# Exponentials added by fours in every attention block

## The chip, the cores and the metric

The kernel runs on one core of one Trainium2 chip. The metric is the device time of one execution in microseconds (us); the time of a kernel is the median of its runs. The engines are TensorE (PE, with its weight loads as PEld), VectorE (DVE), ScalarE (ACT), GpSimd (POOL) and SyncE (SP), which issues DMAs.

## The reference

One pre-layernorm transformer layer in float32, on x of 2 x 1024 x 1024 (2 sequences of 1024 tokens, width 1024), with 32 heads of width 32 and a gated FFN of width 2752:

```python
x = x + attention(layernorm(x))        # softmax(q k^T / sqrt(32)) v per head, then ctx @ ow + ob
h = layernorm(x)
x = x + (silu(h @ W_gate.T) * (h @ W_up.T)) @ W_down.T
```

## The kernel before

**Blocks and units.** Queries are worked on in four blocks of 512: two sequences, two halves each. A *unit* is two heads of one block; a block has 16 units, and `phase` is the number of the block (0 to 3). The keys of a sequence are eight tiles of 128, `kt` = 0 to 7. For each key tile a unit has one buffer `p[kt]` of 128 keys x 1024 (two heads x 512 queries).

**The steps of a unit.** `scores(i)` (L510) makes the scores of two key tiles in psum. DVE keeps a running maximum of them (`largest`, L526), and ACT copies them to `p[kt]` (`keep`, L529). `maximum` turns the maxima into one number per query (L549, L550, a transpose on TensorE at L564, the negated maximum at L565), which goes through DRAM into the tile `m`. Then, tile by tile, `less_maximum` adds `m` to `p[kt]` (L580; on POOL but for some tiles of block 0), `exponential` takes the exponential in place on ACT (L589), and `add` adds an earlier tile's exponentials (L603).

**The additions.** Instead of a sum p0 v0 + p1 v1 the kernel makes p0 (v0 - v1) + (p0 + p1) v1. `differences` replaces v0 by v0 - v1 on POOL (L594), and `add` replaces p1 by p0 + p1. The softmax's denominators are then sums of every second `p`, and half of the matmuls on a column of ones fall away. In block 0 this is done a second time: p3 becomes the sum of four tiles, v1 becomes v1 - v3 (L597), and only tiles 3 and 7 are multiplied by ones. In blocks 1 to 3 tiles 1, 3, 5 and 7 are (`summed`). In those blocks the additions of tiles 1 and 5 are on POOL and those of 3 and 7 on DVE; in block 0 all are on DVE.

**The values.** `values(kt)` (L618) multiplies `p[kt]` by `v`, and for summed tiles by ones, into the psum tile `acc`. A set is four matmuls of 32 output partitions and 256 columns, each of them two instructions on the chip. Values are issued in runs of four tiles (`RUN`), when the last addition of the run has been issued.

**What runs beside attention.** In block 0 it is the projections of q, k and v (L370, L432). Beside block n the output projection (L780) and the FFN of block n - 1 are worked on: gate and up products in groups of four matmuls of 256 columns (L922), down projections in groups of two of 512 columns (L1071), both in a Strassen-like form of seven products. Each group fills one psum tile from a ring of three (`lin`), and DVE or ACT adds it to its place (L936 to L949, L1084, L1086).

**Order.** All instructions are emitted by the program itself. `Emitter` keeps a planned clock: each matmul step adds its planned cost (`MM4` = 855 ns for 512 columns), and the steps of attention are spread evenly over the steps beside them, 128 *beats* to a block. `em.later(d, f)` emits f once the planned clock is d ns on. After `less_maximum(kt)` the exponential comes 3500 ns later and the addition 8100 ns later; in block 0 the second addition comes at 9900 ns. Values follow the run's last `less_maximum` by three beats. The engines take their instructions in the emitted order.

## Time and profile before

| | us |
|---|---|
| median of 3 runs (lowest to highest) | 3282.67 (3280.46 to 3286.37) |
| the profiled execution, and its span | 3281.96, 3280.2 |
| busy: PE, DVE, POOL, ACT | 3217.5, 1920.4, 1758.6, 1431.2 |
| score maxima on DVE, L526 (384 + 64 instructions) | 468.1 + 77.3 |
| values on TensorE, L618, tiles `vals` and `ones` | 266.0, 137.7 |

Busy time is the union of an engine's instructions; the ends of matmuls are modelled and neighbours overlap, so for TensorE the distance from one start to the next tells more than a duration. An arrow in a row (`<-DVE top L526`) names what ended the idle time ahead of those instructions.

### The profile page before, as it was taken

To read this page: it belongs to the slowest core of one execution; us is meant where nothing else is said; L and a number is where in the kernel's file an instruction comes from. 1 tells how busy PE (TensorE), PEld (TensorE's weight loads), DVE (VectorE), ACT (ScalarE), POOL (GpSimd) and SP (SyncE) were. 2 spreads that over 40 slices of the span, in tenths; PEclk is the share of its full clock that TensorE was granted. 3 is DMA by queue.
4 is the path that set the end of the run, shared out by engine and by line. 5 is a ranking of instruction groups with operands and counts; after the bars stand their busy time and mean duration, and the time that the engine had idled before them with its cause. 6 is when DMAs were issued, how large, how long until landed. Compare 5 with 4: busy or idle time off the path is not lost. (4 is left out here: it accounts for less than half of the span.)

```text
span 3280.2 us, 43732 instructions
## 1 busy us (share of the span) xinstructions
PE 3217.5 (98%) x16320; PEld 1801.1 (55%) x16320; DVE 1920.4 (59%) x2478; ACT 1431.2 (44%) x1570; POOL 1758.6 (54%) x871
## 2 busy tenths in 40 slices
PE   8999999999999999999999999989999999999999
PEld 4444444444347655663466556634655566477775
DVE  2265676666356766666666666676666664344334
ACT  2244554444455545563655455545555554010000
POOL 0267776876676655568665555667765665200000
PEclk9999999999999999999999999999999999999999
DMA  4556766655534445446344444463444444544442
GB/s 155 171 184 193 226 192 203 200 180 161 158 99 135 142 151 146 146 146 200 107 142 145 139 141 137 145 192 110 137 145 146 146 138 140 184 151 153 153 152 97
DMA packets 337826, 507.29 MB, mean 155 GB/s; under 512 B 105424, under 2 KB 122064, under 8 KB 337616
## 3 DMA queue, kind: packets, MB, share of 16 engines
q1 hardware_dynamic: 281424, 405.91, 40.3%
q10 hardware_dynamic: 56192, 98.60, 9.8%
q8 instruction: 130, 2.13, 0.3%
q14 instruction: 80, 0.66, 0.1%
HBM read 429.14 MB, written 75.24 MB: 154 GB/s over the span
## 5 line engine op out<-in xcount | busy, mean ns | idle before, releaser
L580 POOL TENSOR_TENSOR p<-p,m 128x1024 f32<-128x1024 f32 x480 | 1180.8, 2483 | 13.6 <-DMA m<-d 13.4
L529 ACT COPY p<-s 128x1024 f32<-128x1024 f32 x512 | 516.7, 1011 | 872.1 <-DVE top L526 664.5
L526 DVE TENSOR_TENSOR top<-s,top 128x1024 f32<-128x1024 f32 x384 | 468.1, 1219 | 289.0 <-PE s L510 280.0
L589 ACT ACTIVATE p<-p 128x1024 f32<-128x1024 f32 x512 | 532.2, 1057 | 234.7 <-POOL p L580 206.8
L922 PE MATMUL p<-sum,m 128*128 128x256 f32 x2688 | 617.8, 383 | 4.9 <-DVE sum L904 3.3
L603 POOL TENSOR_TENSOR p<-p,p 128x1024 f32<-128x1024 f32 x96 | 227.2, 2367 | 658.9 <-ACT p L589 598.3
L922 PEld LDWEIGHTS p<-sum,m 128*128 128x128 f32 x2688 | 503.2, 190 | 124.7 <-issue 43.0
L922 PE MATMUL p<-xn2T,m 128*128 128x256 f32 x2016 | 473.5, 384 | 1.9 <-ACT gate L934 1.3
L370 PE MATMUL pq<-xnT,wqk 128*128 128x512 f32 x1024 | 463.7, 601 | 0.0
L1071 PE MATMUL pd<-wp,h 128*128 128x512 f32 x960 | 442.3, 607 | 8.3 <-DVE x L1084 6.4
L922 PEld LDWEIGHTS p<-xn2T,m 128*128 128x128 f32 x2016 | 378.2, 191 | 98.5 <-issue 45.4
L603 DVE TENSOR_TENSOR p<-p,p 128x1024 f32<-128x1024 f32 x192 | 306.2, 1595 | 134.1 <-ACT p L589 134.0
L370 PEld LDWEIGHTS pq<-xnT,wqk 128*128 128x128 f32 x1024 | 187.2, 190 | 252.8 <-issue 249.0
L1071 PEld LDWEIGHTS pd<-wp,h 128*128 128x128 f32 x960 | 179.3, 193 | 242.5 <-issue 203.4
L510 PE MATMUL s<-q,k 32*128 32x512 f32 x2048 | 300.8, 645 | 7.1 <-ACT p L529 7.0
L1084 DVE TENSOR_TENSOR x<-pd,x 128x512 f32<-128x512 f32 x360 | 236.9, 681 | 86.8 <-PE pd L1071 86.7
L618 PE MATMUL acc<-p,vals 128*32 128x256 f32 x4096 | 266.0, 383 | 1.8 <-DVE p L603 1.8
L1184 POOL TENSOR_TENSOR ws<-raw 128x512 f32<-128x512 f32 x62 | 93.7, 1512 | 299.9 <-DMA raw<-in_w_gu 170.5
L432 PE MATMUL pvv<-wv,xnT 128*128 128x512 f32 x512 | 233.3, 600 | 1.5 <-ACT xnT L266 1.5
L780 PE MATMUL po<-wo,ctx 128*128 128x512 f32 x512 | 234.6, 607 | 0.0
L618 PEld LDWEIGHTS acc<-p,vals 128*32 128x32 f32 x4096 | 120.1, 110 | 143.6 <-issue 70.2
L950 ACT ACTIVATE gate<-gate 128x512 f32<-128x512 f32 x84 | 52.9, 630 | 278.4 <-DVE gate L949 278.0
(96 smaller groups left out, 2451.3 us busy)
## 6 DMA issues: line engine op xcount, KB each, us to landing
m<-dws SPq DMA_DIRECT2D x336, 256.0 KB
m<-in_w_gu SPq DMA_DIRECT2D x252, 256.0 KB
wp<-ddn SPq DMA_DIRECT2D x160, 256.0 KB
m<-d SPq DMA_DIRECT2D x64, 512.0 KB
wp<-in_w_dn SPq DMA_DIRECT2D x120, 256.0 KB
raw<-in_w_gu ACTq DMA_DIRECT2D x84, 256.0 KB
dws<-ws ACTq DMA_DIRECT2D x84, 256.0 KB
x<-in_x SPq DMA_DIRECT2D x32, 512.0 KB
```

The costliest lines, as they stand in the source:

```text
L370: nc.tensor.matmul(ps, wqk[b, g, w, hk][:, k, :], xnT[b, s][:, kc, :], start=(kc == 0), stop=(kc == KC - 1),)
L510: nc.tensor.matmul(ps[a][:, h * NH : (h + 1) * NH], self.k[rows, i * P : (i + 1) * P], self.q[rows, :], start=True, stop=True,)
L526: nc.vector.tensor_tensor(self.top, s, self.p[0] if kt == 1 else self.top, ALU.max)
L529: nc.scalar.copy(self.p[kt], s)
L580: eng.tensor_tensor(p, p, self.m, ALU.add)
L589: nc.scalar.activation(self.p[kt], self.p[kt], AF.Exp, scale=SCALE)
L603: eng.tensor_tensor(self.p[kt], self.p[kt], self.p[kt - back], ALU.add)
L618: nc.tensor.matmul(self.acc[j * HD : (j + 1) * HD, c : c + NQ], w(h), self.p[kt][:, q0 : q0 + NQ], start=start, stop=stop, skip_group_chec ...
L780: nc.tensor.matmul(st["ps"], ctxT[b, blk][:, g, t * P : (t + 1) * P], st["w"][hf, g], start=(g == 0), stop=(g == G - 1),)
L922: nc.tensor.matmul(ps, mats[c, n][:, kc, :], rhs, start=(kc == 0), stop=(kc == hk - 1),)
L1071: nc.tensor.matmul(st["pd"], lefts[n](pi)[:, j, t * P : (t + 1) * P], st["wp", pi, n, j], start=(j == 0), stop=(j == PART // 2 - 1),)
L1084: nc.vector.tensor_tensor(xs, st["pd"], xs, op)
```

## The change

Tiles are added by fours in all four blocks: the second addition, the second difference of `v` and the fewer ones matmuls no longer depend on the phase. The second addition, `add(kt, 2)` for tiles 3 and 7, stands on DVE, since `add` puts tiles 3 and 7 there in every block. The line numbers after `add` move up by four.

```diff
             if kt % 2 == 1:
-                twice = self.phase == 0 and kt % 4 == 3
+                twice = kt % 4 == 3
                 em.later(8100.0, lambda: self.add(kt, 1), None if twice else ("added", self.n, kt))
                 if twice:
                     em.later(9900.0, lambda: self.add(kt, 2), ("added", self.n, kt))
...
             nc.gpsimd.tensor_tensor(v[:, :, 0, :], v[:, :, 0, :], v[:, :, 1, :], ALU.subtract)
-            if self.phase == 0:
-                v = self.v.rearrange("p (i a) n -> p i a n", a=4)
-                nc.gpsimd.tensor_tensor(v[:, :, 1, :], v[:, :, 1, :], v[:, :, 3, :], ALU.subtract)
+            v = self.v.rearrange("p (i a) n -> p i a n", a=4)
+            nc.gpsimd.tensor_tensor(v[:, :, 1, :], v[:, :, 1, :], v[:, :, 3, :], ALU.subtract)
...
-        def summed(self, kt):
-            return kt % (4 if self.phase == 0 else 2) == (3 if self.phase == 0 else 1)
...
-            if self.summed(kt):
+            if kt % 4 == 3:
                 columns(lambda h: ones, NQ, False, kt == NT - 1)
...
-                    cost = MM4 / 2 * (1 + units[k].summed(v))
+                    cost = MM4 / 2 * (1 + (v % 4 == 3))
                     q.add(lambda k=k, v=v: units[k].values(v), cost)
```

## The prediction

> **What bounds the kernel now.** I read the page's first part for shares, then busy time by stage (the windows view), then the timeline of TensorE around one attention step, then the groups by shape, then the runs of down-projection matmuls, where VectorE is fullest.

> ```profile
> PE 3217.5 (98%) x16320; PEld 1801.1 (55%) x16320; DVE 1920.4 (59%) x2478; ACT 1431.2 (44%) x1570; POOL 1758.6 (54%) x871
> ...
> 130.00:900.00 770.00, 763.48 (x3472) 316.32 (x3471) 458.98 (x425) 364.14 (x400) 540.30 (x286) 1.00 0.61 190
> 900.00:1530.00 630.00, 621.23 (x3582) 370.25 (x3581) 409.43 (x544) 334.29 (x357) 390.28 (x185) 0.99 0.48 143
> 1530.00:2180.00 650.00, 627.61 (x3650) 370.05 (x3649) 431.14 (x555) 345.19 (x369) 405.33 (x190) 0.99 0.47 142
> 2180.00:2822.00 642.00, 631.00 (x3614) 374.57 (x3614) 400.62 (x545) 328.34 (x351) 398.98 (x187) 0.99 0.48 145
> 2822.00:3280.00 458.00, 454.35 (x1667) 313.88 (x1665) 182.61 (x340) 27.40 (x54) 17.97 (x15) 1.00 0.45 145
> ```

> The window columns are length, then busy time and instructions of PE, PEld, DVE, ACT, POOL, then granted clock, DMA share, GB/s. The first window shown is the attention of the first block, which runs beside the projections; the next three are the attention of the other three blocks, each beside the output projection and FFN of the block before; the last has no attention. The edit touches the three middle windows alone, 1922 us. There TensorE is busy 621, 628 and 631 us, at a clock of 0.99, and is without work for 9, 22 and 11 us. DVE is busy 65%, 66% and 62%, POOL 62%. So TensorE's own work sets the length, with VectorE the next.

> ```profile
> 1719.20 1.07 PE L618 MATMUL acc<-p,vals 128*32 128x256 f32 x16
> 1720.09 0.61 PE L618 MATMUL acc<-p,ones 128*32 128x256 f32 x8
> 1720.52 1.05 PE L618 MATMUL acc<-p,vals 128*32 128x256 f32 x16
> 1721.39 0.61 PE L618 MATMUL acc<-p,ones 128*32 128x256 f32 x8
> 1721.93 1.98 PE L1071 MATMUL pd<-wp,h 128*128 128x512 f32 x4
> ```

> This is one run of four key tiles. The durations overlap, so cost is read from start to start: a set of 8 instructions on ones takes 1720.52 - 1720.09 = 0.43 us (0.431 by the records in ns), the 16 on values 0.89.

> **The part removed.** A unit is two heads of one block and has two such runs; three blocks of 16 units have 96 runs. Each run loses its first ones set: 96 x 0.431 = 41.4 us of TensorE. The built order agrees: ones matmuls fall from 896 to 512 in the program, 1792 to 1024 on the chip, where each is two instructions. They stand in TensorE's queue between value matmuls and nothing runs under them, so all of it lies on the path. The planner subtracts the same work (half of MM4 per set), so the 128 beats of a block come 13.8 / 128 = 0.11 us closer.

> **The part added.** 96 additions of 128x1024 on DVE, `add(kt, 2)`, and 48 subtractions of 128x128 on POOL.

> ```profile
> L580 POOL TENSOR_TENSOR p<-p,m 128x1024 f32<-128x1024 f32 x480 | 1180.8, 2483 | 13.6 <-DMA m<-d 13.4 <-DVE top L526 0.2
> L603 DVE TENSOR_TENSOR p<-p,p 128x1024 f32<-128x1024 f32 x192 | 306.2, 1595 | 134.1 <-ACT p L589 134.0
> L603 POOL TENSOR_TENSOR p<-p,p 128x1024 f32<-128x1024 f32 x96 | 227.2, 2367 | 658.9 <-ACT p L589 598.3
> L597 POOL TENSOR_TENSOR vals<-vals 128x128 f32<-128x128 f32 x16 | 12.5, 782 | 1.3
> ```

> POOL: 48 x 0.782 = 37.5 us, covered by the 658.9 us that POOL waits at its own additions for an exponential; the path pays nothing. Without that cover it would be 37.5 us of POOL. Queued behind each subtraction are the unit's `less_maximum` steps, so its first exponentials come 0.8 us later, which the same wait swallows.

> DVE: the existing additions take 1201 ns at the least, 1224 in the median, 3442 at the most. Overlaid with POOL's rows, those of 1.2 us have no POOL operation running, and the long ones start inside one; POOL's `less_maximum` likewise goes from 2.36 to 3.4 us after an addition. The second addition is planned 1.8 us after the first, where POOL was busy in about one case of six, so I take 1.4 us (between 1.2 and 3.44, near the low end by that count): 96 x 1.4 = 134 us of DVE, and by the mean of the row, 1.6, it is 153. DVE goes from 64% to about 72% of these blocks. No engine overflows on average; what counts is lateness.

> [...]

> Who is behind the added instruction? On DVE its queue holds the evictions of TensorE's small psum tiles (three buffers) and the score maxima; on TensorE the value matmuls of tiles 3 and 7 wait for it. I priced three lateness terms from start and end times in the trace.

> (a) Values. From the end of the last addition to the matmuls that read it there are 4.5 to 5.9 us in the medians of the three blocks. Shifting that end by 1.2 us would stall TensorE 1.2 us in all 96 runs together; by 1.8 us, 2.4; by 2.4 us, 4.6; by 3.0 us, 8; by 3.6 us, 15.7. The planned distance is 1.8 us and mostly one or two operations stand between the two additions. I take 4.6, bounds 1 and 16.

> (b) Down-projection runs (L1071). There are 15 beside attention; I show three.

> ```profile
> 1166.00:1199.00 33.00, 32.03 (x133) 12.97 (x132) 28.59 (x37) 15.24 (x16) 16.36 (x7) 1.00 0.43 131
> 1709.00:1746.00 37.00, 34.71 (x179) 14.19 (x179) 31.45 (x37) 17.44 (x19) 17.64 (x9) 1.00 0.45 138
> 2581.00:2613.00 32.00, 31.53 (x131) 12.73 (x130) 27.17 (x38) 15.63 (x17) 17.79 (x8) 1.00 0.43 133
> ```

> ```profile
> 1714.20 2.47 DVE L1084 TENSOR_TENSOR x<-pd,x 128x512 f32<-128x512 f32 x4
> 1716.60 0.67 DVE L1040 TENSOR_TENSOR s<-h 128x512 f32<-128x512 f32 x1
> 1717.20 0.67 DVE L1084 TENSOR_TENSOR x<-pd,x 128x512 f32<-128x512 f32 x1
> 1717.80 1.21 DVE L603 TENSOR_TENSOR p<-p,p 128x1024 f32<-128x1024 f32 x1
> 1718.93 2.54 DVE L526 TENSOR_TENSOR top<-s,top 128x1024 f32<-128x1024 f32 x2
> 1721.38 0.68 DVE L1084 TENSOR_TENSOR x<-pd,x 128x512 f32<-128x512 f32 x1
> ```

> DVE is at 87%, 85% and 85% here, against 64% over the blocks, and in the timeline it runs without a break: an addition put after 1719 delays every eviction behind it. About 25 of the 96 additions fall into these runs. A psum tile is wanted again by the third group after it; a quarter of the groups have under 0.7 to 1.3 us to spare there, half have 1.8 to 2.5. So 25 x 1.4 = 35 us of delay meets slack of its own size, and I let half pass: 17 us. Bounds: 5 us, if it lands in gaps, and 25 x 1.6 = 40, if all of it passes.

> (c) Elsewhere, 71 additions. A gate/up group (L922) has 2.4 us to spare in three cases of four. If every one of its evictions were late by 0.8 us, TensorE would lose 11 us over the three blocks, by 1.6 us 44; late time after an addition lasts some 4 us, 71 x 4 = 284 us of the 1400 outside (b), one fifth. That gives 2 to 9; I take 5. The score tiles have 4.4 to 5.1 us to spare in the median and give nothing. The negated maximum (L565), which the second addition of tile 3 precedes, and the DMA of `m` behind it come about 1.4 us later; POOL waits 13.4 us for that DMA in the whole kernel, and again at its additions for longer, so this is nothing too. No DMA is moved past another.

> Sum: -41.4 + 4.6 + 17 + 5 = -14.8 us. A stall by one of these lets DVE catch up, so (a) and (b) partly count the same lateness; I drop 2 us for it and forecast -17. The profiled execution took 3281.96 us, its span 3280.2 with 1.8 around it, and lies 0.7 us under the median of the three runs, 3282.67. 3282 - 17 = 3265.

> **The rivals.**
> First, the lateness is all absorbed and the whole 41.4 us is gained: 3240.6. For it: DVE idles over a third of these blocks, and 152 us of its idle time there ends at a score matmul, which is room. In the first block, where the same form already runs, TensorE lost 6.5 us in 770. Against: down-projection runs do not exist there, and its groups are four times as long.
> Second, slower: in the down-projection runs VectorE becomes the engine that sets the pace. All of (b) passes at the mean price, 40 us, with (a) at 8 and (c) at 5: 3282 - 41.4 + 53 = 3294. It decides from where (a) to (c) together exceed 41.4 us, that is, with (a) and (c) at 13, when some 18 of the 25 additions there pass whole at 1.6; that DVE leaves only 13 to 15% free there speaks for it, that TensorE loses no more than 1 to 2 us per run today against it.
> Third, no change: middle prices at each place, (a) 15.7, (b) 17, (c) 9 add up to 41.7: 3282. That the change does not do what it says is excluded by the counts of the built order.

> **How the numbers follow.** Differences of 0.2%, 6.6 us, are about what a measurement of this kernel can tell. The forecast, half the gain lost, has 0.48; the full gain 0.22; no change 0.13; slower 0.17. Both gaining cases together give 0.70 for faster. The order of work also shifts with the closer beats, and the three blocks' idle of 9, 22 and 11 us shows that such order alone is worth several us. The range runs from the full gain, 3240, to 3288, half way between no change and the slower case; about 0.1 lies above it and little below.

> **What would show it.** L618 on ones x1024; L603 on DVE x288 near 1.4 to 1.6 us each; the three blocks' windows some 5 us shorter each; longer waits of `pd L1071` on `x L1084` and of `acc L618` on `p L603`. I am wrong in (b) if the L1071 runs are no longer in time than before, in (a) if `acc L618` waits for over 16 us, and in the price if the added additions take 2 us or more.

## The result and the profile after

| | before | after |
|---|---|---|
| median of 6 runs, us (lowest to highest) | 3282.19 (3277.36 to 3286.37) | 3300.57 (3291.68 to 3306.74) |
| ratio of the runs, 95% interval | | 1.0052 (1.0033 to 1.0070) |
| profiled execution, span, us | 3281.96, 3280.2 | 3301.26, 3299.5 |
| mean granted clock of TensorE | 0.994 | 0.989 |

The change makes the kernel slower by 0.5%, 18 us. The prediction was 3265 us with a range up to 3288. First the page's busy times, with the groups of additions and values:

```profile
PE 3194.0 (97%) x15552; PEld 1774.6 (54%) x15552; DVE 2080.3 (63%) x2574; ACT 1432.3 (43%) x1570; POOL 1815.7 (55%) x919
...
L602 DVE TENSOR_TENSOR p<-p,p 128x1024 f32<-128x1024 f32 x288 | 483.4, 1679 | 121.1 <-ACT p L589 121.0
...
L614 PE MATMUL acc<-p,vals 128*32 128x256 f32 x4096 | 254.4, 384 | 40.9 <-DVE p L602 40.7
```

TensorE has 768 instructions less and is busy 23.5 us less, though the kernel is longer. VectorE has 96 additions more. The last row holds what is new: ahead of the value matmuls TensorE is idle for 40.9 us, and the additions ended it. In the kernel before the same group was idle for 1.8 us, and its down projections waited 7.1 us (columns of the second row: total, times, longest, us):

```profile
L618 PE MATMUL acc<-p,vals 128*32 128x256 f32 x4096 | 266.0, 383 | 1.8 <-DVE p L603 1.8
```

```profile
PE pd L1071 <- DVE x L1084: 7.1, 12, 1.4
```

The longest waits of TensorE at the blocks' steps in the kernel after, in the same columns:

```profile
PE acc L614 <- DVE p L602: 40.7, 24, 7.7
PE top L564 <- DVE part L550: 15.0, 9, 3.5
PE pd L1067 <- DVE x L1080: 12.4, 16, 1.8
```

The down projections wait 12.4 us; the wait for `part` was 16.1 before. The stages, in the columns of the prediction's windows, with the blocks' new ends:

```profile
905.00:1530.00 625.00, 600.89 (x3276) 356.70 (x3275) 462.90 (x568) 329.38 (x353) 400.44 (x196) 0.98 0.47 141
1530.00:2190.00 660.00, 629.65 (x3423) 365.87 (x3423) 473.65 (x591) 349.12 (x372) 426.03 (x208) 0.98 0.47 142
2190.00:2840.00 650.00, 620.06 (x3363) 365.46 (x3362) 454.10 (x575) 328.17 (x351) 413.76 (x201) 0.99 0.46 142
```

VectorE is busy 72% of the three blocks, as forecast. TensorE idles for 24, 30 and 30 us in them, and the clock is a hundredth lower in two. The worst wait, at the end of block 1, on TensorE, then on VectorE, then on GpSimd:

```profile
1518.66 1.50 PE L614 MATMUL acc<-p,vals 128*32 128x256 f32 x24
1527.84 1.08 PE L614 MATMUL acc<-p,vals 128*32 128x256 f32 x8 [7.68 <-DVE p L602]
```

```profile
1520.52 1.23 DVE L602 TENSOR_TENSOR p<-p,p 128x1024 f32<-128x1024 f32 x1 [5.02 <-ACT p L589]
1521.66 0.68 DVE L1005 TENSOR_TENSOR x<-pd,x 128x512 f32<-128x512 f32 x1
1522.26 1.22 DVE L526 TENSOR_TENSOR top<-s,top 128x1024 f32<-128x1024 f32 x1
1523.39 1.10 DVE L1025 TENSOR_TENSOR x<-x,x 128x512 f32<-128x512 f32 x1
1524.42 3.37 DVE L602 TENSOR_TENSOR p<-p,p 128x1024 f32<-128x1024 f32 x1
```

```profile
1520.58 9.43 POOL L580 TENSOR_TENSOR p<-p,m 128x1024 f32<-128x1024 f32 x3
```

TensorE has issued tiles 0 to 2 (24 instructions) and stands at tile 3. The first addition began at 1520.52, late because its exponential was late; three operations stand between it and the second, which then takes 3.37 us beside POOL's `less_maximum` steps (L580). TensorE starts again at 1527.84, just behind it. In windows laid around this wait the third figure from the end is the granted clock:

```profile
1517.00:1524.40 7.40, 3.16 (x29) 1.10 (x27) 3.88 (x4) 1.48 (x2) 7.32 (x6) 1.00 0.74 264
1524.40:1531.20 6.80, 3.36 (x18) 1.44 (x19) 4.59 (x4) 4.76 (x6) 6.80 (x3) 0.50 0.16 36
1531.20:1538.00 6.80, 6.80 (x22) 2.70 (x21) 4.59 (x6) 3.04 (x4) 6.80 (x4) 1.00 0.34 128
```

The clock is halved (0.50) from 1524.4 to 1531.2, so the matmuls behind the wait are slow as well: in the halved stretches of this trace the down projections (L1067) start 853 ns apart in the median, elsewhere 429. By the clock records the kernel before has 10 such stretches of 3.4 or 6.8 us, the kernel after 16 (the last of each is cut off by the kernel's end).

An account by starts, from 905 us to the last value matmuls: I add up how much later than usual each TensorE instruction starts, that is, the distance from the start before it less the median for the same two groups and the same place in its run of matmuls. Before, that gives 77 us, after 136. Of the 59 us more, 42 stand at value matmuls that TensorE waited ahead of (1.6 and 43.8), 8 in other matmuls inside stretches of halved clock (19.9 and 28.2), 9 elsewhere. Less the 41 us of work removed this leaves 18 us, as measured.

### The profile page after: what moved, and what is told of

The parts are those of the page before. It is cut to its first block, busy times and chain, and to the rows that moved or that the text cites. A ratio compares the mean times of both kernels' runs of the same rounds, so it can differ in the third digit from the quotient of the medians.

```text
span 3299.5 us, 42366 instructions
## 1 busy us (share of the span) xinstructions
PE 3194.0 (97%) x15552; PEld 1774.6 (54%) x15552; DVE 2080.3 (63%) x2574; ACT 1432.3 (43%) x1570; POOL 1815.7 (55%) x919
## 3 DMA queue, kind: packets, MB, share of 16 engines
q8 instruction: 124, 2.03, 0.3%
## 5 line engine op out<-in xcount | busy, mean ns | idle before, releaser
L580 POOL TENSOR_TENSOR p<-p,m 128x1024 f32<-128x1024 f32 x480 | 1207.5, 2538 | 9.9 <-DMA m<-d 8.6
L589 ACT ACTIVATE p<-p 128x1024 f32<-128x1024 f32 x512 | 533.6, 1057 | 254.7 <-POOL p L580 227.1
L526 DVE TENSOR_TENSOR top<-s,top 128x1024 f32<-128x1024 f32 x384 | 467.8, 1218 | 257.5 <-PE s L510 249.7
L602 DVE TENSOR_TENSOR p<-p,p 128x1024 f32<-128x1024 f32 x288 | 483.4, 1679 | 121.1 <-ACT p L589 121.0
L1067 PE MATMUL pd<-wp,h 128*128 128x512 f32 x960 | 445.2, 609 | 12.5 <-DVE x L1080 12.4
L1067 PEld LDWEIGHTS pd<-wp,h 128*128 128x128 f32 x960 | 179.0, 193 | 248.9 <-issue 202.3
L614 PE MATMUL acc<-p,vals 128*32 128x256 f32 x4096 | 254.4, 384 | 40.9 <-DVE p L602 40.7
```

The source lines that it names most:

```text
L526: nc.vector.tensor_tensor(self.top, s, self.p[0] if kt == 1 else self.top, ALU.max)
L580: eng.tensor_tensor(p, p, self.m, ALU.add)
L589: nc.scalar.activation(self.p[kt], self.p[kt], AF.Exp, scale=SCALE)
L602: eng.tensor_tensor(self.p[kt], self.p[kt], self.p[kt - back], ALU.add)
L614: nc.tensor.matmul(self.acc[j * HD : (j + 1) * HD, c : c + NQ], w(h), self.p[kt][:, q0 : q0 + NQ], start=start, stop=stop, skip_group_chec ...
L1067: nc.tensor.matmul(st["pd"], lefts[n](pi)[:, j, t * P : (t + 1) * P], st["wp", pi, n, j], start=(j == 0), stop=(j == PART // 2 - 1),)
```

## The experiments

Theory A is that TensorE waits for the second addition at the value matmuls; its rival B that VectorE is too full, or held up beside GpSimd ("locked" in the expectations: in blocks 1 to 3 of the kernel before, 36 of the 96 additions on VectorE start while a POOL operation runs, and end 1.08 to 1.09 us after it), so that evictions are late. C, which came up after experiment 4, is that VectorE's queue is stopped wherever the additions stand and the waits only move. Ratios are to the kernel before on the same chip, with their 95% intervals. The experiments ran on several chips, where the kernel before took 3282 to 3287 us, so a difference of two medians can be off by a few us.

**1. Without the second additions.**

```diff
-                    em.later(9900.0, lambda: self.add(kt, 2), ("added", self.n, kt))
+                    second = (lambda: self.add(kt, 2)) if self.phase == 0 else (lambda: None)
+                    em.later(9900.0, second, ("added", self.n, kt))
```

> The changed kernel without its second additions in blocks 1 to 3 (the sums of four are then sums of two: that part of the computation is left out). It prices the removed half by itself. Both theories, value matmuls waiting for the second addition (A) and VectorE too full or locked by GpSimd (B), expect the whole removed TensorE work as gain: 3282 - 41 = 3241 us. If it stays above 3265, the loss has a third cause, such as the new order or the subtraction on GpSimd.

3248.23 us, ratio 0.9885 (0.9868 to 0.9903): 38 us faster than before, close to the 41.4 of the prediction. The subtractions on POOL are in this kernel, so they cost little or nothing. The whole loss of 52 us (3300.6 - 3248.2) comes with the second additions. But the value matmuls already wait a little for the first ones:

```profile
PE acc L615 <- DVE p L603: 6.2, 3, 3.3
```

**2. Value matmuls a beat later.**

```diff
-            k, kt = divmod(n - NT - LAG - 3, NT)
+            k, kt = divmod(n - NT - LAG - 4, NT)
```

> The changed kernel with each run of value matmuls one beat (about 5 us) later in TensorE's order; every addition stays. A: the 44 us that TensorE waits ahead of tile 3 and tile 7 go, so about 3300 - 42 = 3258 us. B: the additions still cost what they cost, 3290 us or more, with the waits now ahead of the down projections.

3298.73 us, 1.0050 (1.0032 to 1.0067). It settles nothing: the last run of each unit now stands behind the load of the next v into its buffer, so it multiplies that v and TensorE waits for the load:

```profile
PE pd L1067 <- DVE x L1080: 23.6, 23, 2.2
PE acc L614 <- DMA vals<-dv: 20.4, 7, 5.2
```

**3. The load alone, on the kernel before.** 96 additions into a spare tile, at 9900 ns.

```diff
                     em.later(9900.0, lambda: self.add(kt, 2), ("added", self.n, kt))
+                elif kt % 4 == 3:
+                    em.later(9900.0, lambda: nc.vector.tensor_tensor(spare, twin, twin, ALU.add))
```

> The kernel before with 96 additions of 128x1024 more on VectorE, at the place of the second additions, on operands that nobody waits for. All other work is that of the kernel before. A: evictions late by what the prediction's terms (b) and (c) gave, 10 to 20 us: 3292 to 3302 us. B: the load itself is the loss of about 60 us: 3342 us.

3295.18 us, 1.0032 (1.0021 to 1.0044): 11 us, within what (b) and (c) of the prediction allow. The spare additions read one constant tile twice and write bf16, so they are not the second additions in every respect; at 1392 ns in the mean they took the 1.4 us of the prediction.

**4. Both additions together.**

```diff
-                    em.later(9900.0, lambda: self.add(kt, 2), ("added", self.n, kt))
+                    em.later(9900.0 if self.phase == 0 else 8100.0, lambda: self.add(kt, 2), ("added", self.n, kt))
```

> The changed kernel with the second addition of blocks 1 to 3 planned at 8100 ns, directly behind the first, in place of 9900. The last addition then ends about 1.5 us after the first in place of 3.05. A: most of the 44 us of waits go, some 15 are left: about 3272 us. B: the same work on VectorE at nearly the same time, 3300 us.

3332.44 us, 1.0148 (1.0133 to 1.0164), the opposite of what A expected. The waits at values were halved, and others took their place:

```profile
PE p L918 <- DVE neg L565: 19.9, 12, 3.8
PE acc L614 <- DVE p L602: 18.4, 10, 6.2
PE pd L1067 <- DVE x L1080: 16.1, 18, 2.8
```

The negated maximum (L565), often between the two additions in the changed kernel, now stands behind both; it holds one of the three small psum tiles, and the gate/up products wait for that tile (2.7 us in the changed kernel). VectorE takes its instructions in the emitted order: in the worst wait of the changed kernel the maximum of 1522.26 (L526) had its scores at 1514.24 and the maximum before it at 1515.50, and stood behind the addition that began at 1520.52. In this run VectorE waits 118.4 us for an exponential that an addition needs; every eviction behind such an addition waits too.

**5 to 7. The softmax a beat earlier.** After; before; and after with the additions at 10500 and 13000 ns.

```diff
-    LAG = 3
+    LAG = 2
...
-            k, kt = divmod(n - NT - LAG - 3, NT)
+            k, kt = divmod(n - NT - LAG - 4, NT)
```

> The changed kernel with the subtraction of the maximum, the exponentials and all additions one beat (5 us) earlier, while scores and value matmuls keep their places. Theory A (the loss is TensorE waiting for the second addition): the 44 us of waits go, 3300 - 44 = 3256 us or somewhat less. Theory B (VectorE too full, locked by GpSimd): 96 additions are still there and delay evictions, so 3290 us or more. Third theory C, from the run with both additions together: the additions block VectorE's queue wherever they stand, and waits only move: 3280 to 3300 us.

> The control: the same move by one beat on the kernel before. It had 1.6 us of waits at value matmuls, so A expects no change, 3284 us, give or take 5 for the new order. If it gains as much as the changed kernel does, the move helps by something else than the second addition.

> As the first of these, and the two additions of tiles 3 and 7 of blocks 1 to 3 planned at 10500 and 13000 ns in place of 8100 and 9900, so that VectorE's queue is not stopped by an addition whose exponential is not there yet. A: no waits at values in either, so 3256 us as the first. C: evictions behind the first addition no longer wait, some 10 us better than the first.

3361.46, 3332.42 and 3348.13 us; 1.0236 (1.0212 to 1.0259), 1.0163 (1.0133 to 1.0193), 1.0199 (1.0155 to 1.0242). The control loses 1.6%, so the move has a price of its own. `m` is not there a beat earlier: POOL, which waited 13.4 us for it in the kernel before, has this among its waits in the first of these, and 286.8 us in the control:

```profile
POOL p L580 <- DMA m<-d: 265.9, 48, 11.8
```

No wait at values is left in it, as A expected, but with this new wait nothing can be concluded on the time. How much of the 1.6% is that wait was not separated.

**8. A short second addition.**

```diff
-            eng.tensor_tensor(self.p[kt], self.p[kt], self.p[kt - back], ALU.add)
+            w = 64 if back == 2 and self.phase else S
+            eng.tensor_tensor(self.p[kt][:, :w], self.p[kt][:, :w], self.p[kt - back][:, :w], ALU.add)
```

> The changed kernel with the second addition of blocks 1 to 3 on 64 of 1024 columns (the rest of that addition is left out). Order, dependency and waits in the queue stay, the load of 134 us goes to some 15. A with position (what lies between the two additions makes them late): the last addition ends about 1.7 us after the first in place of 3.05, waits at values fall to about 10 us: 3262 us. If the length of the addition itself is all: 3250 us. If the queue behind the first addition is the cause whatever the second costs: 3285 us.

3268.58 us, 0.9952 (0.9935 to 0.9969). The short additions took 366 ns each, 35 us in all, and ended 1.97 us after the first additions in the mean. The time lies between the case with position and the case of the queue. The dependency and the place in the queue cost 20 us over the kernel without second additions, with little load, and they show as waits at values:

```profile
PE acc L615 <- DVE p L603: 23.4, 11, 7.6
```

The other 32 us come with the length.

**9 and 10. Value matmuls a beat later, with the buffers for it**, on the changed kernel and on the one before.

```diff
-    RING = NT + LAG + RUN + 4
+    RING = NT + LAG + RUN + 5
...
-                if kt == NT - 2:
+                if kt == NT - 1:
                     q.add(units[k].load_v, needs=("v", units[k].b, units[k].hf))
...
-            k, kt = divmod(n - NT - LAG - 3, NT)
+            k, kt = divmod(n - NT - LAG - 4, NT)
```

> The changed kernel with each run of value matmuls one beat (about 5 us) later, with one more buffer for the exponentials (paid by one buffer less, 9 for 10, for the weights on 128x512 tiles) and with the load of a unit's v one beat later too; scores, softmax and additions keep their places. A (the loss is TensorE waiting at the value matmuls, and the lower clock after such waits): 44 us of waits and some 12 us of halved clock go, 3300 - 50 = 3250 us. C (waits only move): 3280 to 3300 us, with longer waits at evictions.

> The control: the same buffers and the same later value matmuls on the kernel before, where 1.6 us were waited at value matmuls. A: no change, 3282 us give or take 5. If it moves by more, the buffers or the new place of the matmuls are worth that much by themselves, and the run above is to be read against this one.

3289.05 us, 1.0014 (0.9997 to 1.0031), and 3285.17 us, 1.0007 (0.9996 to 1.0018). The control is unmoved. In the changed kernel the waits at values are gone, but only about 12 us of the 50 that A expected came back. The first waits of its list:

```profile
PE pd L1067 <- DVE x L1080: 25.2, 26, 2.2
...
PE p L918 <- ACT gate L930: 10.6, 8, 3.0
```

Evictions are now what is late (12.4 us in the changed kernel for the first row, 10.9 in the control). So C was right in part: TensorE waits for the same late VectorE at another place.

**11. Running sums.** Each of tiles 1, 2 and 3 adds the tile before it, tiles 2 and 3 on VectorE.

```diff
-            if kt % 2 == 1:
+            if self.phase > 0:
+                if kt % 4 > 0:
+                    em.later(8100.0, lambda: self.add(kt, 1), ("added", self.n, kt))
+            elif kt % 2 == 1:
...
-            eng = nc.vector if self.phase == 0 or kt % RUN == RUN - 1 else nc.gpsimd
+            eng = nc.vector if self.phase == 0 or kt % RUN >= RUN - 2 else nc.gpsimd
```

> The changed kernel with running sums in blocks 1 to 3: tile 1 gets tile 0's sum, tile 2 tile 1's, tile 3 tile 2's, and v becomes v0 - v1, v1 - v2, v2 - v3, v3. It has as many additions on VectorE (two to a run) and as few ones matmuls as the changed kernel, but only one addition follows the last exponential of a run. A: the waits at values fall to the 2 to 6 us of the kernel before and of the one without second additions, the load of some 11 us stays: 3248 + 11 = 3259 us. B and C: as many additions on VectorE, so 3290 to 3300 us.

3371.56 us, 1.0276 (1.0253 to 1.0299), the worst of all. No wait at values is among its long ones, yet TensorE waits 58.4 us at down projections. The wait, and the additions:

```profile
PE pd L1075 <- DVE x L1088: 58.4, 28, 5.1
```

```profile
L610 DVE TENSOR_TENSOR p<-p,p 128x1024 f32<-128x1024 f32 x288 | 575.9, 1999 | 135.5 <-ACT p L592 115.7 <-POOL p L610 19.5
```

The same number of additions cost 576 us in place of 483, since the new place of tile 2's addition falls mostly among POOL's `less_maximum` steps: 91 of its 96 additions start while a POOL operation runs, and they take 2.49 us in the mean. In the changed kernel 54 of the 96 first additions and 21 of the 96 second ones start so, and 72 of these 75 end 1.08 to 1.12 us after the POOL operation that ran. Another 19.5 us of VectorE go to waiting for POOL's own addition, and POOL has 48 subtractions more. Where the addition stands mattered here as much as how many there are.

**12. The load without the dependency, on the changed kernel.** Experiment 1 with a spare addition in place of nothing.

```diff
-                    second = (lambda: self.add(kt, 2)) if self.phase == 0 else (lambda: None)
+                    spared = lambda: nc.vector.tensor_tensor(spare, twin, twin, ALU.add)
+                    second = (lambda: self.add(kt, 2)) if self.phase == 0 else spared
```

> The changed kernel with its second additions of blocks 1 to 3 replaced, in the same place of VectorE's order, by additions of the same size that nobody waits for (so the sums of four are left out). Same load and same TensorE work as the changed kernel, no dependency. If the dependency of the value matmuls is the loss (A): 3248 + 11 = 3259 us. If the load costs more where TensorE has less to do (B): 3280 us or more.

3276.69 us, 0.9976 (0.9966 to 0.9986): between A and B, and 28 us above the kernel without second additions. The load costs 28 here and 11 in experiment 3. The dependency makes the rest, 24 us (3300.6 - 3276.7). TensorE waits at the evictions here, and hardly at the values:

```profile
PE pd L1071 <- DVE x L1084: 19.2, 21, 2.9
...
PE acc L618 <- DVE p L606: 3.9, 5, 1.4
```

This kernel has 22 us of halved time, as much as the kernel before; the changed one has 39. So the added stretches of halved clock came with the dependency on an addition of full length and are in its 24 us (experiment 8, with the short one, has 24 us of halved time).

**13. Experiment 9 without the second additions.**

> The kernel with later value matmuls, one buffer more for exponentials and one fewer for weights, without the second additions of blocks 1 to 3 (sums of four left out). A and B: 3248 + 3 = 3251 us, the control's 3 us on top of the kernel without second additions. If it is 3270 or more, the later value matmuls cost time of their own in the shorter kernel, and the 3289 us were not the additions.

3255.16 us, 0.9911 (0.9896 to 0.9926), 4 us above what both expected. So in experiment 9 the additions cost 34 us (3289 - 3255) though no value matmul waits for them.

**14 and 15. The second additions on GpSimd**, with the later value matmuls of experiment 9, and without them.

```diff
-            eng = nc.vector if self.phase == 0 or kt % RUN == RUN - 1 else nc.gpsimd
+            eng = nc.vector if self.phase == 0 or (kt % RUN == RUN - 1 and back == 1) else nc.gpsimd
...
-                    em.later(9900.0, lambda: self.add(kt, 2), ("added", self.n, kt))
+                    em.later(9900.0 if self.phase == 0 else 11000.0, lambda: self.add(kt, 2), ("added", self.n, kt))
```

The second part is in 14 alone.

> As the changed kernel with later value matmuls, but the second additions of blocks 1 to 3 on GpSimd, planned at 11000 ns. VectorE has the load of the kernel before; GpSimd gets 96 x 2.4 = 227 us more. B: 3251 us, or a little above. A: 3251 us too unless the sums come late again. If GpSimd's queue now delays the exponentials: 3285 us or more.

> The changed kernel with the second additions of blocks 1 to 3 on GpSimd, planned at 9900 ns as before; value matmuls at their place, buffers as in the changed kernel. Taken off VectorE, the 28 us of load go, but each second addition takes 2.4 us in place of 1.45, in a queue that also waits for exponentials. If the dependency is a cost of its own, waits at values stay or grow: 3270 to 3300 us. If the load was all, 3248 us.

With both: 3240.30 us, 0.9866 (0.9851 to 0.9880), which is 44 us (3282.2 x 0.0134): the 41.4 us of the removed matmuls and a little more, and faster than either kernel. On GpSimd alone: 3269.96 us, 0.9960 (0.9946 to 0.9973). The waits of TensorE at values and at down projections, without and with the later matmuls:

```profile
PE acc L614 <- POOL p L602: 48.6, 14, 12.3
...
PE pd L1067 <- DVE x L1080: 6.5, 12, 1.2
```

```profile
PE acc L614 <- POOL p L602: 19.9, 5, 7.3
...
PE pd L1067 <- DVE x L1080: 8.2, 19, 0.9
```

With the load off VectorE the down projections wait 6.5 and 8.2 us, about as before the change. On GpSimd alone the dependency still costs 22 us (3270.0 - 3248.2).

Experiment 14 is also 15 us faster than experiment 13, which leaves the second additions out. So its 44 us are not simply the removed matmuls at no price: TensorE still waits 19.9 us at values, and other things became cheaper. Its halved time is 19.7 us against 28.8, and fewer of VectorE's first additions started beside a POOL operation (28 of 96 against 56). Why this order of work is the better one was not tried.

**Where TensorE is late.** The account by starts of the section on the result, in us, for the runs that the argument rests on. Smaller groups are in the total alone, and the last column holds only what the other columns don't:

| run | total | at values | down projections | gate and up | halved clock |
|---|---|---|---|---|---|
| before | 77 | 2 | 16 | 22 | 20 |
| 3, load on the kernel before | 90 | 4 | 23 | 22 | 20 |
| after | 136 | 44 | 24 | 26 | 28 |
| 1, no second additions | 87 | 6 | 26 | 23 | 16 |
| 8, short second additions | 105 | 24 | 29 | 21 | 17 |
| 12, load, no dependency | 110 | 4 | 35 | 30 | 20 |
| 9, values later | 134 | 0 | 49 | 35 | 31 |
| 13, values later, no second additions | 105 | 0 | 29 | 23 | 30 |
| 14, values later, GpSimd | 90 | 19 | 29 | 18 | 14 |

## Why the prediction was wrong

**The part removed** was right: 41.4 us forecast, 38 measured alone (experiment 1), and 44 with experiment 14, other waits included.

**POOL's subtractions** were rightly taken as nearly free: they are in experiment 1, which misses the 41.4 us by some 3. They took 574 ns in place of 782.

**The addition's price.** A spare addition took 1.39 us and the second additions of the blocks 1.45, against 1.4 forecast. The whole row grew by (483.4 - 306.2) / 96 = 1.85 us for each addition put in, since the first additions became longer as well (1.94 us in place of 1.62 in these blocks). VectorE's 72% was right, and so was the point that lateness counts and not the average.

**Term (a), the values, is the step that failed.** It held 4.6 us, bounds 1 and 16. By time the dependency costs 24 us (after against experiment 12; 20 in experiment 8), and TensorE waits 40.7 us at `acc` for the additions, where the prediction had named 16 as the sign of being wrong. The wait itself was foreseen; its size was not, for two reasons. The first is the shift. From the end of the first addition to the end of the second there are 3.05 us in the mean of the 96 runs (1.60 between them, 1.45 for the second), where I took the row of 2.4; and it lies between 1.3 and 7.0 us, where I moved all runs by the same. The second is the slack, which I read from the kernel before. In experiment 1, which has the changed order without the second additions, tile 3's matmuls start 4.04 us behind the end of the first addition in the mean, against 5.03 before: they come 0.43 us earlier in the run, since the ones set ahead of them is gone, and the beats are closer. The table made again from the trace of experiment 1 gives 27 us for a shift of 3.0, where the prediction's gives 8, and 37 us if each run is moved by its own shift in the changed kernel. The two largest waits, 7.7 and 6.4 us, stand at ends of blocks where the first addition was already late: VectorE had waited 5.0 and 3.8 us for its exponential.

**Terms (b) and (c)**, 22 us for the load, were about right where I used them: 28 us in the kernel with less TensorE work. That the same load costs 11 us in the kernel before was not foreseen. By the account both have some 7 to 9 us more at the down projections; the kernel with less TensorE work has 7 more at the gate and up products and 5 in halved clock as well, the kernel before none. That its 41 us more of TensorE work give the evictions more room is a likely reason, not shown. The picture behind (b) was wrong in part, for in the changed kernel itself the down projections hardly wait (12.4 against 7.1 us).

**The overlap** of the terms, for which 2 us were dropped, is therefore the larger matter. From experiment 12 to the changed kernel the account has 40 us more at values and 8 more in halved clock, but 11 less at down projections and 4 less at gate and up products: TensorE stops at the values, and VectorE catches up meanwhile. Waits at values and at evictions take each other's place, and repairing one alone (4, 9, 15) gave back part or nothing.

**The sum.** The forecast missed by 35 us. As far as medians of several chips can be added, 19 of it are (a), 6 the load, 3 the part removed, and the 2 that were dropped; some 5 stay unexplained.

**A term was missing**: the stretches of halved clock, 39 us of full clock in place of 22. They are part of what the dependency cost.

**The rivals.** The slower rival had the sign and nearly the size (3294 against 3300.6), but by luck: its place, the down projections, is not where this kernel lost. The full gain rested on room on VectorE; it came when the second addition was taken off VectorE and the value matmuls came a beat later, and in part with fewer stretches of halved clock.

What stays open: why the load reaches the gate and up products in one kernel and not in the other, and why experiment 14 beats experiment 13.

## What to carry to other kernels

To price an operation put into the queue of an in-order engine that another engine waits for, look at the worst runs and not at median slack, take the slack where the change has already moved things, and let everything that the change itself moves eat into that slack: the consumer that comes earlier, the operations between, the producer that is already late. Load and dependency are two prices, and removing one only shows the other; here a gain of the whole size came when the addition went to the engine with room and its consumer was placed a beat later. Before a step is moved, look at what it waits for there: a beat earlier cost 1.6% in a kernel where no step had changed.

## What the runs showed of the hardware

```profile
1820.64 0.33 PE L564 MATMUL top<-ident,part 128*128 128x128 f32 x1 [2.03 <-DVE part L550]
1821.84 4.69 PE L1071 MATMUL pd<-wp,h 128*128 128x512 f32 x7 [0.87 <-DVE x L1084]
```

Of the 3.4 us ahead of 1821.3 TensorE was idle for some 2.4: the wait of 2.03 us and the first part of the next. Not every such wait was followed by one, and its place counted: in each profile all halved stretches inside the kernel begin on one grid of 3.413 us, and a wait of 2.04 us from 1645.61 on in the same kernel, which this grid divides into 1.63 and 0.41 us, was followed by full clock (1.00). In the profiles before and after, counted from 130 us on with the modelled ends of matmuls, 18 steps of that grid at full clock have TensorE idle for over 2.0 us, and all 18 are followed by a halved one; of the 23 halvings 3 follow a step with under 1.7 us idle. My count over all seventeen profiles gives 191 of 192 steps, and 18 of 238 halvings. The halved time takes 22 us of full clock in the kernel before, 39 in the changed one and 64 with running sums, and is 19.7 in the fastest.

In the changed kernel 146 of the 288 additions of 128x1024 on VectorE started while no POOL operation ran; they took 1.21 us in the mean and none over 1.23. The 54 first additions of blocks 1 to 3 that started beside one took 2.51 us in the mean, and the second addition of the worst wait 3.37; this one ended 1.08 us after the POOL operation beside which it started. With other places for the additions, and 48 subtractions more on POOL, the mean of all of them went from 1679 to 1999 ns at the same count (experiment 11).
